# Six blocks of a shared expert taken in pairs, with stage 2 on its own after every two units

## The chip, the cores and the metric

The kernel runs on one core of a Trainium2 chip, in fp32. The metric is the device time of one execution in microseconds. Three executions of the kernel before took 1153.5, 1155.28 and 1156.86 us; the median is 1155.28 us. A further execution was recorded by the profiler; it took 1156.11 us.

The engines are named as in the profile: PE is the matrix engine TensorE, PEld its loading of weights, DVE is VectorE, ACT is ScalarE, POOL is GpSimd, and SP is SyncE, which here issues most of the DMAs.

## The reference

The input is `x` of 4 sequences x 1024 tokens x 512 features, and one condition vector of 512 for each sequence. Two residual layers follow one another:

```python
# layer 0: a linear map whose input is scaled by the condition
ys = cond / sqrt(512);  d = rsqrt((ys * ys) @ (W * W) + eps)
x  = x + ((x * ys) @ W) * d
# layer 1: a mixture of 8 routed experts, 2 for each token, and a shared one
shared = (silu(xf @ w1) * (xf @ w3)) @ w2            # 512 -> 1024 -> 512
s      = sigmoid(concat([xf, tf]) @ router_W)         # (4096, 8)
topk_idx = top_k(s + router_bias, 2)
gates  = s_sel / (s_sel.sum() + 1e-9)
h      = gelu(xf @ W1e[e]);  y = h @ W2e[e]           # 512 -> 512 -> 512
x      = x + (shared + sum of gates * y) / 3
```

The part that the change touches is `shared`, for 3072 of the 4096 tokens.

## The kernel before

**Blocks and phases.** The 4096 tokens are `NB` = 8 blocks of `TB` = 512. Layer 0 and the logits of the router run first, to about 132 us. Then comes the shared expert of the first six blocks (`early` = 6; blocks 6 and 7 are kept for the end), from 132 to 565 us. Meanwhile the router's choices are worked out on DVE and the tokens' rows are sorted by expert through DRAM. The routed experts follow (class `Double`, which does two groups of 256 rows at once, and class `Slot`), to about 1003 us, and last the two late blocks of the shared expert, under which the routed rows are gathered back.

**Seven products.** Every matrix product is cut in 2 x 2 blocks and made of seven block products instead of eight, as Strassen and Winograd do. Products 1, 6, 5 and 3 are added one after another in one PSUM bank, the chain, which is read out between them; products 2, 7 and 4 go to other banks (2 in one, 7 and later 4 in another). The sums of blocks that the scheme needs (of weights, of tokens, of hidden values) are made on DVE: `weight_sums` (L435), `token_sums` (L418), `hidden_sums` in `Shared`, `out_sums` (L897).

**A unit.** `Shared(blk, u)` takes one block and 256 of the 1024 hidden columns, of both `w1` (the gate, i = 0) and `w3` (the value, i = 1); there are four units a block (`HU` = 4). In stage 1 the two halves of the token side are the first and last 256 tokens of the block (`LO`, `HI`), and a bank of 512 columns holds the gate in one half and the value in the other. So each of the seven products is 2 matrices x 2 pieces of the contraction (`KH` = 2) = 4 matmuls of 256 columns. ACT copies the chain out (`evict`, L985), DVE adds the other banks (`add`, L989), ACT applies silu, and DVE multiplies gate and value to the hidden values.

**Stage 2** of a unit (`parts`, `seconds`, `drain`, L1052 to L1092) is the product with `w2`, 14 matmuls of 256 columns. It is cut in four parts, which `Shared.rest` (L991) issues between the products of the next unit's stage 1. Products 2, 7 and 4 of stage 2 add up over the four units of a block in PSUM; the chain is drained into the tiles `base` (which begin with x) four times in each unit, the three others once in each block, by DVE's `scalar_tensor_tensor` at L1092.

**What sets the order.** The order is written out by hand (`tc.manual_schedule()`): each engine runs its instructions in the order in which the program emits them, and waits by semaphores for the data. In every unit there are two points, `task(2 * self.at)` and `task(2 * self.at + 1)`, at which the program emits whatever the table `tasks` (L1573 to L1625) names for that point:

- the router's work: `sigmoid`, `pick_first`, `pick_second`, `count` (L735), `across`, `slots_of_experts` (L751), `positions`, `take_positions`, `gates`, `norm_gates`;
- sums of weights and of tokens for later units;
- DMAs on SP: `fetch_pairs` loads `base`, `fill` clears the sorted rows, `stage_rows` brings rows in, `fetch_first`, `fetch_second` and `load_rows` bring weights and rows of the first experts; on ACT's queue, `clear_rows`; on POOL's, `move_rows`, which scatters rows by index after a small copy on DVE;
- transposes (`turn_half`, L1153) and sums for the first `Double`.

**PSUM.** There are eight banks: four in the pool `ps_a`, handed out in turn (`bank_a`), used by stage 1, and four single ones, b0 to b3 (`bank_b`), used by stage 2 and, before it, by the logits: the logits of a block by chunk (`logits_by_chunk`, L376, tile `pq`) and their sum over chunks (`fold_logits`, L393, tile `pr`), to which DVE adds the condition's share at L399.

**The first Double.** `Double.rest` (L1251 on) issues the stage 2 of the unit before it, there the last `Shared` unit of block 5, between its own products, like `Shared.rest`. The driver's loop over all units is L1627 to L1670.

Of the kernel before, what the change touches and what calls it, by code (L numbers as in the profile page):

```python
# [45 lines left out]
def kernel(  # L46
# [328 lines left out]

    def logits_by_chunk(blk):  # L376

        pq = bank_b(f"pq{blk}")
        for k in range(KC):
            nc.tensor.matmul(  # L380
                pq[ts(k, Q)],
                lhsT=rw_pad[:, k, :],
                rhs=x1T[blk][:, k, :],
                start=True,
                stop=True,
                tile_position=(0, k * Q),
            )
        partial[blk] = late2.tile([P, TB], FP, tag="partial", name=f"partial{blk}")
        nc.scalar.activation(partial[blk], pq, AF.Copy)
# [2 lines left out]

    def fold_logits(blk, s):  # L393
        if s == 0:
            prs[blk] = bank_b(f"pr{blk}")
        nc.tensor.matmul(prs[blk][:, ds(s * E, E)], lhsT=partial[blk][:, ts(s, P)], rhs=fold, start=True, stop=True)
        if s == NS - 1:
            b = blk // BPB
            nc.vector.tensor_tensor(  # L399
                score[:, ts(blk, NS), :],  # L400
                prs[blk][:, : NS * E].rearrange("p (s e) -> p s e", e=E),
                t_logit[:, b : b + 1, :].to_broadcast([P, NS, E]),
                ALU.add,
            )
# [13 lines left out]
    def token_sums(blk):  # L418
        b = x1T[blk]
        k1, k2 = slice(0, KH), slice(KH, KC)  # L420
        v = t_tiles[blk % 2].rearrange("p (n k t) -> p n k t", n=3, k=KH)
        t1, t2, t4 = (v[:, n] for n in range(3))
        sub = lambda o, i0, i1: nc.vector.tensor_tensor(o, i0, i1, ALU.subtract)
        if blk not in begun:
            token_sum(blk)
        nc.vector.tensor_tensor(t2, b[:, k1, HI], b[:, k1, LO], ALU.add)
        sub(t1, b[:, k2, HI], t2)
        sub(t4, b[:, k2, LO], t2)
        t_of[blk] = (t1, t2, b[:, k1, HI], t4)

    def s_views(i, u):
        n = KH * P
# [163 lines left out]
    for blk in range(NB):  # L596
# [65 lines left out]
        if blk == early - 1:  # L662
            weight_sums(0)
        if blk == early:
            token_sums(0)
        if blk == NB - 1:
            weight_sums(1)
            nc.gpsimd.memset(zeros, 0.0)
# [12 lines left out]
    def open_pools():  # L681
        lin_ctx.close()
        later["row"] = ctx.enter_context(tc.tile_pool(name="row", bufs=4))
        sums = ctx.enter_context(tc.tile_pool(name="sums", bufs=1))
        more = sums.tile([P, 10 * TH], FP, name="more")
        work = ctx.enter_context(tc.tile_pool(name="work", bufs=1))
        t_tiles.append(sums.tile([P, 3 * KH * TH], FP, name="t1"))
        hgh = work.tile([P, 4, 2 * TB], FP, name="hgh")
        spot = [hgh[:, 3, ts(n, TH)] for n in range(4)]
        later["hs"] = spot[:3]  # L690
        later["more"] = [more[:, ts(n, TH)] for n in range(10)] + [spot[3], falling.rearrange("p t e -> p (t e)")]
        wide2 = lambda ap: ap.rearrange("p (q t) -> p q t", q=2)
        later["h2"] = [hgh[:, 2 * i : 2 * i + 2, :].rearrange("p q (m t) -> p q m t", m=2) for i in range(2)]
        later["s_w"] = [more[:, ts(n, 2 * TH)].rearrange("p (k q c) -> p k q c", k=KH, q=2) for n in range(3)]
        later["s_h"] = [wide2(more[:, ts(n, 2 * TH)]) for n in (3, 4)] + [wide2(zeros)]
        later["both"] = [hgh[:, i : i + 2, :].rearrange("p i (m t) -> p i m t", m=2) for i in range(2)]
        later["g"] = hgh[:, 1, :]
        later["h"] = [hgh[:, 2 * i, :] for i in range(2)]
# [193 lines left out]
    def out_tiles(u):  # L892
        return later["more"][3 * u : 3 * u + 3]
# [3 lines left out]
    def out_sums(u):  # L897
        t1, t2, t4 = out_tiles(u)
        b1, b2 = w2_sb[:, 2 * u, :], w2_sb[:, 2 * u + 1, :]
        b11, b12, b21, b22 = b1[:, LO], b1[:, HI], b2[:, LO], b2[:, HI]  # L900
        if u not in summed:
            nc.vector.tensor_tensor(b12, b22, b12, ALU.subtract)
            summed.add(u)
        nc.vector.tensor_tensor(t2, b12, b11, ALU.add)
        nc.vector.tensor_tensor(t1, b22, t2, ALU.subtract)
        nc.vector.tensor_tensor(t4, b21, t2, ALU.subtract)

    class Shared:

# [230 lines left out]
    def fetch_weights(j):  # L1140
        fetch_first(j)
        fetch_second(j)
# [16 lines left out]
    class Double:  # L1159
# [99 lines left out]
        def rest(self, prev, task):  # L1259
            j, h = self.j, later["h2"][self.j % 2]  # L1260
            self.h = h
            parts = [lambda mm=mm, drain=drain: (mm(), drain()) for mm, drain in prev.parts()]
            following = None if self.last else units[self.at + 1]
            self.evict(0, LO)
            self.product(self.chain, 6, False)
# [15 lines left out]
            parts[1]()  # L1281
            if following:
                following.sums_of_tokens((3, 2, 1))
            self.product(self.chain, 3, False)
            nc.scalar.activation(h[:, :, 0, HI], self.chain, AF.Gelu)
            nc.scalar.activation(h[:, :, 0, LO], h[:, :, 0, LO], AF.Gelu)
# [1 line left out]
            if following:  # L1288
                following.sums_of_first()
            task(2 * self.at)  # L1290
            self.product(self.seven, 4, False)
            self.add(self.seven, 1, LO)
            nc.scalar.activation(h[:, :, 1, :], h[:, :, 1, :], AF.Gelu)
            self.sums_of_second()
# [232 lines left out]
    def open_slot_pools():  # L1527
        rt_ctx.close()
        slot = ctx.enter_context(tc.tile_pool(name="slot", bufs=1))
        xg0 = slot.tile([P, KC, GS], FP, name="xg0")  # L1530
        xg1 = t_tiles[1][:, : KC * GS].rearrange("p (k t) -> p k t", k=KC)
        later["xg"] = [xg0, xg1]
        later["segs"] = slot.tile([P, 3 * SEGS, P], FP, name="xsegs")
        later["xseg"] = [later["segs"][:, ts(i, SEGS), :] for i in range(3)]

# [16 lines left out]
            nc.vector.transpose(big[0][:, k, :], later["segs"][:, : TB // Q, ts(k, Q)])  # L1552
        fetch_pairs(last_blk, [spare_pair(m) for m in range(2)])

    units = [Shared(blk, u) for blk in range(early) for u in range(HU)]
    units += [Double(j) for j in range(PAIRED)]
    units += [Slot(j) for j in range(SINGLE, SURE)]
    late = len(units)
    units += [Shared(blk, u) for blk in range(early, NB) for u in range(HU)]

    for i, unit in enumerate(units):
        unit.at = i
    tasks = {i: [] for i in range(2 * len(units))}

    def run_tasks(i):
# [5 lines left out]
        nc.scalar.dma_start(out=ys_d[ds(SURE * GS + i * P, P)], in_=zeros)  # L1571

    for u, work in (  # L1573
        (0, [lambda: out_sums(0)]),
        (1, [lambda: weight_sums(3, (0,))]),
        (2, [lambda: weight_sums(3, (1,)), lambda: out_sums(1)]),
        (3, [sigmoid, pick_first]),
        (4, [pick_second]),
        (5, [lambda: out_sums(2), count]),
        (6, [across, slots_of_experts]),  # L1580
        (7, [lambda: out_sums(3), positions]),
        (8, [load_spare, take_positions]),
        (9, [gates]),
        (10, [norm_gates]),
        (8 * HU + 1, [lambda: fetch_weights(0)]),
        (6 * HU + 4, [open_slot_pools]),
        (10 * HU + 1, [lambda: fetch_first(2)]),
        (10 * HU + 4, [lambda: fetch_second(2)]),
        (10 * HU + 4, [lambda: turn_half(0), lambda: load_rows(3)]),
        (10 * HU + 5, [lambda: turn_half(1), lambda: load_rows(4)]),  # L1590
        (10 * HU + 6, [lambda: units[early * HU].sums_of_first((1, 2))]),
        (10 * HU + 7, [lambda: units[early * HU].sums_of_tokens((3, 2))]),
        (10 * HU + 7, [lambda: units[early * HU].sums_of_first((7, 4))]),
        (10 * HU + 7, [lambda: units[early * HU].sums_of_tokens((1, 4))]),
        (2 * late, [reload_last, lambda: out_sums(0)]),
        (2 * late + 1, [lambda: out_sums(1)]),
        (2 * late + 3, [lambda: out_sums(2)]),
        (2 * late + 6, [lambda: out_sums(3)]),
        (2 * late - 1, [lambda: token_sum(early)]),
        (2 * late + 3, [turn_last]),  # L1600
        (2 * late + 5, [lambda: token_sums(last_blk)]),
        (2 * (late + HU + 1), [reload_w2]),
    ):
        tasks[u] += work
    for i in range((NSLOT - SURE) * SUB):
        tasks[6 * HU + 4 + i].append(lambda i=i: clear_rows(i))
    for i in range(ROWS // FILL):
        tasks[1 + i // 2].append(lambda i=i: fill(i))
    for m in range(NT // 2):
        tasks[9 + 2 * m].append(lambda m=m: stage_rows(m))  # L1610
        for i in range(2):
            tasks[10 + 2 * m + i].append(lambda t=2 * m + i: move_rows(t))
    for j in range(3):
        tasks[10 * HU + 2 + j].append(lambda j=j: load_rows(j))
    for blk in range(1, early):
        tasks[2 * blk * HU - 3].append(lambda blk=blk: token_sums(blk))
    for blk in range(early):
        tasks[2 * blk * HU].append(lambda blk=blk: fetch_pairs(blk))
    mine = list(range(early * NS))
    mine = [early * NS + i for i in range(NS)] + mine[:-NS] + list(range(NT - NS, NT)) + mine[-NS:]  # L1620
    points = 4 * TAIL * HU
# [4 lines left out]

    for s in range(NS):  # L1627
        fold_logits(NB - 2, s)
    units[0].begin()
    logits_by_chunk(NB - 1)  # L1630
    units[0].sevens()
    for s in range(NS):
        fold_logits(NB - 1, s)
    weight_sums(2)
    open_pools()
    prev = None
    for u, unit in enumerate(units):
        if u == late:
            for n in tc.Switch(later["spare"], E):
                prev.end = SURE + n  # L1640
# [19 lines left out]
        if u == late:  # L1660
# [1 line left out]
            base[early] = [spare_pair(2), pair_tile("base1")]  # L1662
            token_sums(early)
            unit.sevens()
        if prev is None:
            unit.rest(prev, run_tasks, units[u + 1])
        else:
            unit.rest(prev, run_tasks)
# [41 lines left out]
```

## Time and profile before

| what | value |
|---|---|
| median of three executions | 1155.28 us (1153.5 to 1156.86) |
| profiled execution | 1156.11 us, its span 1154.3 us |
| PE busy in the span | 1135.5 us (98%), 5222 records |
| DVE busy | 735.1 us (64%), 1533 instructions |
| ACT busy | 246.5 us (21%), 455 instructions |
| POOL busy | 181.8 us (16%), 222 instructions |
| granted PE clock, mean | 0.997 |
| first matmul of the first early unit | 132 us |
| first matmul of the first Double | 565 us |

The span is the time from the first to the last instruction in the profile; the execution's own time is 1.8 us more. The busy time of an engine is the sum of its instructions; an fp32 matmul leaves two records on PE and two weight loads. Names like L940 are lines of the kernel; L940 is the matmul of stage 1 and L1076 that of stage 2, in all eight blocks. In the timeline, equal neighbouring instructions are drawn together as "x8", and a square bracket behind a line tells how long the engine stood idle before it and which engine, tile and line let it go.

### The profile page before, as it was taken

What the parts mean: (1) busy time and instruction counts of PE and PEld (TensorE: products, weight loads), DVE (VectorE), ACT (ScalarE), POOL (GpSimd) and SP (SyncE); (2) the same over time, 40 slices, a digit from 0 to 9 for tenths busy, and PEclk for the clock granted to TensorE, in tenths of its full rate; (3) what the DMA queues carried; (4) which work ended last, traced back from release to release, by engine and by line L of the source; (5) the groups of instructions that cost most, each with busy time, mean ns of one, the idle gap of its engine ahead of it and who ended that gap; (6) DMA issues with size and microseconds to landing.
All of it is one profiled execution on the core that took longest, in us unless ns stands there. A gap on an engine that the chain in (4) does not pass through costs nothing. (4 is left out here: it accounts for less than half of the span.)

```text
span 1154.3 us, 14608 instructions
## 1 busy us (share of the span) xinstructions
PE 1135.5 (98%) x5222; PEld 974.4 (84%) x5222; DVE 735.1 (64%) x1533; ACT 246.5 (21%) x455; POOL 181.8 (16%) x222
## 2 busy tenths in 40 slices
PE   9899999999999999999999999999999998999998
PEld 6588888888888888888888888888888887888886
DVE  4688777854545445454687766677635554379987
ACT  2133231111111111111122222222222221121111
POOL 2000000022212222120000000000201100086850
PEclk9999999999999999999999999999999998999999
DMA  9698698322433337444356776657789983198971
GB/s 172 121 204 198 174 394 325 110 74 110 146 110 128 109 128 249 144 154 101 66 128 166 207 182 157 164 156 211 183 204 243 234 231 112 66 268 296 300 262 73
DMA packets 139393, 203.68 MB, mean 176 GB/s; under 512 B 9892, under 2 KB 67364, under 8 KB 139304
## 3 DMA queue, kind: packets, MB, share of 16 engines
q1 hardware_dynamic: 113096, 142.77, 44.6%
q0 software_dynamic: 14784, 47.24, 12.9%
q10 hardware_dynamic: 11424, 12.59, 3.8%
q8 instruction: 44, 0.72, 0.3%
q14 instruction: 45, 0.37, 0.1%
HBM read 120.76 MB, written 81.79 MB: 175 GB/s over the span
## 5 line engine op out<-in xcount | busy, mean ns | idle before, releaser
L1092 DVE SCALAR_TENSOR_TENSOR base<-s,base 128x512 f32<-128x512 f32 x131 | 88.7, 687 | 77.5 <-PE s L1076 77.4
L1076 PE MATMUL s<-w_sb,hgh 128*128 128x256 f32 x496 | 122.7, 380 | 1.9 <-DVE base L1092 1.9
L985 ACT ACTIVATE hgh<-ch 128x512 f32<-128x512 f32 x96 | 57.3, 596 | 273.8 <-PE ch L940 266.0
L878 POOL DMA_INDIRECT x1s_d<-big,addr x64 | 64.3, 1005 | 320.0 <-DVE addr L877 310.2
L1076 PEld LDWEIGHTS s<-w_sb,hgh 128*128 128x128 f32 x496 | 94.0, 190 | 16.1 <-DVE base L1092 3.5
L989 DVE TENSOR_TENSOR hgh<-se,hgh 128x512 f32<-128x512 f32 x64 | 44.1, 689 | 71.2 <-ACT hgh L985 62.3
L1512 POOL DMA_INDIRECT big<-ys_d,addr x64 | 71.8, 1122 | 104.9 <-DVE addr L1511 87.4
L125 POOL DMA_DIRECT2D xsegs<-x1s_d x40 | 23.2, 588 | 388.3 <-DVE big L1157 296.5
L1076 PE MATMUL s<-more,hgh 128*128 128x256 f32 x316 | 81.3, 380 | 0.9 <-DVE xsegs L1092 0.9
L1357 DVE TENSOR_TENSOR yd<-d,yd 128x512 f32<-128x512 f32 x36 | 24.8, 690 | 71.4 <-ACT yd L1353 39.1
L1076 PEld LDWEIGHTS s<-more,hgh 128*128 128x128 f32 x316 | 59.9, 190 | 9.6 <-DVE xsegs L1092 1.3
L1340 PE MATMUL d<-big,hgh 128*128 128x256 f32 x288 | 66.1, 379 | 0.0
L940 PE MATMUL ch<-w0t,seg 128*128 128x256 f32 x256 | 61.0, 381 | 1.0 <-ACT hgh L985 1.0
L1340 PEld LDWEIGHTS d<-big,hgh 128*128 128x128 f32 x288 | 54.8, 190 | 7.4
L940 PE MATMUL ch<-t,seg 128*128 128x256 f32 x256 | 60.5, 379 | 0.0
L940 PEld LDWEIGHTS ch<-w0t,seg 128*128 128x128 f32 x256 | 48.3, 190 | 8.9 <-ACT hgh L985 2.6
L940 PEld LDWEIGHTS ch<-t,seg 128*128 128x128 f32 x256 | 48.7, 190 | 6.5
L940 PE MATMUL se<-big,w_sb 128*128 128x256 f32 x224 | 53.0, 380 | 0.0
L940 PE MATMUL ch<-big,w_sb 128*128 128x256 f32 x224 | 53.0, 380 | 0.0
L940 PE MATMUL ch<-big,seg 128*128 128x256 f32 x224 | 52.9, 379 | 0.0
L940 PE MATMUL tw<-big,w_sb 128*128 128x256 f32 x224 | 52.9, 379 | 0.0
L940 PEld LDWEIGHTS se<-big,w_sb 128*128 128x128 f32 x224 | 42.6, 190 | 6.5 <-issue 0.8
(300 smaller groups left out, 2129.9 us busy)
## 6 DMA issues: line engine op xcount, KB each, us to landing
big<-in_L_cond_W1e_dram SPq DMA_DIRECT2D x88, 256.0 KB, 5.8
big<-in_L_cond_W2e_dram SPq DMA_DIRECT2D x22, 1024.0 KB, 5.6
x1s_d<-w0t SPq DMA_DIRECT2D x13, 1536.0 KB, 16.8
xsegs<-x1s_d SPq DMA_DIRECT2D x96, 128.0 KB, 3.2
ys_d<-yd SPq DMA_DIRECT2D x24, 512.0 KB, 4.3
x_d<-back SPq DMA_DIRECT2D x32, 256.0 KB, 4.4
big<-x_d SPq DMA_DIRECT2D x16, 512.0 KB, 3.7
base<-x_d SPq DMA_DIRECT2D x12, 512.0 KB, 4.6
```

Source lines behind the costliest of these rows:

```text
L125: eng.dma_start(out=tile_ap[ts(g, Q)], in_=v[g])
L878: ins = nc.gpsimd.indirect_dma_start(out=x1s_d, out_offset=bass.IndirectOffsetOnAxis(ap=at.bitcast(U32), axis=0), in_=staged(t // 2)[:, t ...
L940: nc.tensor.matmul(out, lhsT=lhs[:, k, :], rhs=rhs[:, k, :], start=start and k == 0, stop=k == KH - 1, skip_group_check=not start,)
L985: nc.scalar.activation(self.both[:, :, m, cols], self.chain, AF.Copy)
L989: nc.vector.tensor_tensor(r, bank, r, ALU.add)
L1076: nc.tensor.matmul(out[:, s], lhsT=a[:, ts(s, P)], rhs=b, start=start and s == 0, stop=True, skip_group_check=not (start and s == 0),)
L1092: nc.vector.scalar_tensor_tensor(r, bank, third, r, ALU.mult, ALU.add)
L1340: nc.tensor.matmul(out[:, i], lhsT=a[:, q, ts(i, P)], rhs=b[:, q, :], start=start and i == 0 and q == 0, stop=q == 1, skip_group_check=not ...
L1357: nc.vector.tensor_tensor(r, bank, r, ALU.add)
L1512: nc.gpsimd.indirect_dma_start(out=picks[t][i], out_offset=None, in_=ys_d, in_offset=bass.IndirectOffsetOnAxis(ap=at.bitcast(U32), axis=0) ...
```

## The change

The six early blocks are taken as three pairs. A new class `Pass` takes one matrix (the gate of unit u, then its value) for two blocks at once: the two halves of the token side in stage 1 are now the two blocks of the pair, 512 tokens each, instead of the halves of one block. A pass has 14 matmuls of 512 columns; there are 24 passes. Between its own chain products it issues products 1 and 2 of the next pass. Its banks are pinned: the chain takes b0 and b3 in turn, product 2 takes b1, products 7 and 4 take b2. The sums over the two blocks (`both_sums`) replace `token_sums` for these blocks.

Stage 2 no longer lies between the products of a stage 1. After every two units (four passes) a `Second` for each of the two blocks does it for both units at once: 28 matmuls of 256 columns, with seven drains on DVE. The first is begun in the fourth pass, by two halves of products 1 and 2 in the place of the next pass's; `Second.run` does the rest of the first block with pieces of the second between, and `Second.parts` does what is left of the second. Stage 2 takes its banks from `ps_a`, and adds nothing up in PSUM over more than two units.

The points for tasks are now 72 rounds, 24 for each pair and 12 for every two units: eight in the four passes, two in `run`, two in `parts`. Tasks are placed anew on them; `sigmoid` stands on round 4, `count` with half of `weight_sums(3)` on 7, `across` and `slots_of_experts` on 9. `weight_sums(2)`, which stood ahead of the first unit, becomes two tasks. The `base` tiles of both blocks of a pair are fetched together. Tiles are laid out anew (`hgh` has six rows instead of four; `more` nine tiles instead of ten), and the last logits take bank b3.

The first `Double` has no stage 2 of another unit to issue between its products, and issues its product 4 ahead of its product 3. The late blocks stay in class `Shared`.

```diff
     def logits_by_chunk(blk):
-        pq = bank_b(f"pq{blk}")
+        pq = bank_b(f"pq{blk}", 3 if blk == NB - 1 else None)
...
-            prs[blk] = bank_b(f"pr{blk}")
+            prs[blk] = bank_b(f"pr{blk}", 3 if blk >= NB - 2 else None)
...
+    def both_sums(p, names):
+        a, b = x1T[2 * p], x1T[2 * p + 1]
+        sub = lambda o, i0, i1: nc.vector.tensor_tensor(o, i0, i1, ALU.subtract)
+        for n, k in names:
+            if n == 3:
+                sub(b[:, k, :], b[:, KH + k, :], b[:, k, :])
+            if n == 2:
+                nc.vector.tensor_tensor(both_t(2, k), b[:, k, :], a[:, k, :], ALU.add)
+            if n == 1:
+                sub(both_t(1, k), b[:, KH + k, :], both_t(2, k))
+            if n == 4:
+                sub(both_t(4, k), a[:, KH + k, :], both_t(2, k))
...
+    class Pass:
...
+        def product(self, out, n, start):
+            u, w = self.u, w13[self.i]
+            a, b = x1T[2 * self.p], x1T[2 * self.p + 1]
...
+                1: (w[:, :KH, c1], lambda k: a[:, k, :]),
+                2: (w[:, KH:, c1], lambda k: a[:, KH + k, :]),
+                3: (s4, lambda k: b[:, KH + k, :]),
+                4: (w[:, KH:, c2], lambda k: both_t(4, k)),
+                5: (s1, lambda k: both_t(1, k)),
+                6: (s2, lambda k: both_t(2, k)),
+                7: (w[:, :KH, c2], lambda k: b[:, k, :]),
...
+        def rest(self, fillers, task, following=None, closing=None):
+            if not self.taken:
+                self.evict(0, 0)
+            self.product(self.chain, 6, False)
+            if not self.has_seven:
+                self.sevens()
+            self.add(self.two, 0, 0)
+            self.evict(1, 0)
+            fillers[0]()
+            task()
+            self.product(self.chain, 5, False)
+            self.evict(1, 1)
+            self.add(self.seven, 1, 1)
+            fillers[1]()
+            self.product(self.chain, 3, False)
+            self.close(0, ts(0, TB))
+            self.close(0, ts(1, TB), self.chain)
+            if closing:
+                closing.sum(3)
+            self.product(self.seven, 4, False)
+            self.add(self.seven, 1, 0)
+            if following:
+                following.evict(0, 0)
+                following.taken = True
+                self.close(1, slice(0, 2 * TB))
+            else:
+                self.close(1, ts(0, TB))
+                self.close(1, ts(1, TB))
+            task()
+
+    class Second:
...
+        def run(self, other, task):
+
+            self.first(1)
+            self.drain(self.chain, 0, LO)
+            self.seven = self.bank("ss")
+            self.product(self.seven, 7, True)
+            self.sum(1)
+            self.sum(2)
+            self.second(1)
+            other.first(0)
+            self.product(self.chain, 6, False)
+            self.drain(self.two, 0, LO)
+            self.drain(self.chain, 1, LO)
+            task()
+            other.first(1)
+            self.drain(self.seven, 1, HI)
+            self.product(self.chain, 5, False)
+            self.sum(4)
+            self.drain(self.chain, 1, HI)
+            other.sum(3)
+            self.product(self.seven, 4, False)
+            other.sum(1)
+            other.sum(2)
+            self.product(self.chain, 3, False)
+            self.drain(self.seven, 1, LO)
+            other.drain(other.chain, 0, LO)
+            self.drain(self.chain, 0, HI)
+            other.sum(4)
...
+            task()
...
+        def seconds(self, part):
+            if part == 0:
+                self.seven = self.bank("ss")
+                self.product(self.seven, 7, True)
+            if part == 1:
+                self.product(self.chain, 6, False)
+                self.second(0)
+                self.second(1)
+            if part == 2:
+                self.product(self.chain, 5, False)
+            if part == 3:
+                self.product(self.seven, 4, False)
+                self.product(self.chain, 3, False)
+
+        def take(self, part):
+            if part == 0:
+                self.drain(self.seven, 1, HI)
+            if part == 1:
+                self.drain(self.chain, 1, LO)
+                self.drain(self.two, 0, LO)
...
     class Double:
...
+            if not prev:
+                self.product(self.seven, 4, False)
             self.product(self.chain, 3, False)
...
+    on(4, sigmoid, pick_first)
+    on(5, lambda: weight_sums(2, (1,)), pick_second)
+    on(7, count, lambda: weight_sums(3, (0,)))
+    on(9, across, slots_of_experts)
...
+    for p in range(PAIRS):
+        on(p * ROUND + 2, lambda p=p: fetch_pairs(2 * p), lambda p=p: fetch_pairs(2 * p + 1))
+        if p + 1 < PAIRS:
+            on(p * ROUND + 18, lambda p=p: both_sums(p + 1, ((3, 0), (3, 1))))
+            on(p * ROUND + 20, lambda p=p: both_sums(p + 1, ((2, 0), (2, 1))))
+            on(p * ROUND + 21, lambda p=p: both_sums(p + 1, ((1, 0), (1, 1))))
+            on(p * ROUND + 22, lambda p=p: both_sums(p + 1, ((4, 0), (4, 1))))
...
+    on(68, lambda: turn_half(0), lambda: load_rows(3))
+    on(69, lambda: turn_half(1), lambda: load_rows(4))
...
+    for at, one in enumerate(passes):
+        if at % 4 == 0 and at > 0:
+            one.begin()
+        if not one.closes:
+            nxt = passes[at + 1]
+            one.rest((nxt.begin_chain, nxt.begin_two), next_round, following=nxt)
+            continue
+        two = [Second(2 * one.p + i, one.u - 1) for i in range(2)]
+        one.rest((lambda: two[0].first(0), lambda: two[0].second(0)), next_round, closing=two[0])
+        two[0].run(two[1], next_round)
+        for i, (mm, drain) in enumerate(two[1].parts()):
+            mm()
+            drain()
+            if i in (1, 3):
+                next_round()
```

## The prediction

> **What bounds the kernel now.** I read the page first: engines, then stretches of the span, then single instructions.
>
> ```profile
> span 1154.3 us, 14608 instructions
> PE 1135.5 (98%) x5222; PEld 974.4 (84%) x5222; DVE 735.1 (64%) x1533; ACT 246.5 (21%) x455; POOL 181.8 (16%) x222
> ```
>
> TensorE (PE) is busy 98% of the span, so only two things move the time: what a matmul takes, and whether PE stands still. The table of stretches (from:to, length, then busy time and count of PE, weight loads, DVE, ACT, POOL, then granted clock, DMA share, GB/s) says so of the stage that is changed, which runs from 131 to 565 us:
>
> ```profile
> 350.00:400.00 50.00, 50.00 (x233) 44.08 (x232) 22.57 (x49) 8.11 (x17) 9.89 (x11) 1.00 0.32 111
> 131.00:590.00 459.00, 457.40 (x2127) 400.92 (x2126) 267.93 (x598) 84.87 (x157) 64.85 (x65) 1.00 0.46 155
> ```
>
> 50.00 of 50 us busy: here PE never waits, and all other work is hidden. In 131 to 590 only 1.6 us are idle. The timeline (start, length of the group, what it is; in brackets the idle time before it and its releaser) shows where, and gives the prices of waits:
>
> ```profile
> 49.49 0.67 PE L527 MATMUL chl<-t_lin,x1T 128*128 128x256 f32 x2 [2.60 <-DVE x1T L488]
> ...
> 135.60 1.07 PE L380 MATMUL pq<-x1T,rw_pad 128*32 128x512 f32 x8
> 136.27 0.18 DVE L399 TENSOR_TENSOR score<-pr,t_logit 128x32 f32<-128x32 f32 x1
> ...
> 147.95 1.89 PE L940 MATMUL se<-w0t,w_sb 128*128 128x256 f32 x8
> 150.01 1.13 PE L940 MATMUL ch<-w0t,seg 128*128 128x256 f32 x4 [0.17 <-ACT hgh L985]
> ...
> 166.78 1.28 ACT L716 ACT_TABLE_LOAD   x1
> 169.03 0.92 PE L940 MATMUL ch<-w0t,seg 128*128 128x256 f32 x3 [0.63 <-ACT hgh L985]
> ...
> 189.17 0.61 DVE L737 TENSOR_TENSOR picked<-one,two 128x256 f32<-128x256 f32 x1
> 190.83 0.69 DVE L415 TENSOR_TENSOR big<-big 128x512 f32<-128x512 f32 x1
> ...
> 199.51 0.16 DVE L755 TENSOR_TENSOR shift<-pp,last 128x8 f32<-128x8 f32 x1
> 203.20 0.67 DVE L989 TENSOR_TENSOR hgh<-se,hgh 128x512 f32<-128x512 f32 x1
> ...
> 303.40 1.03 PE L1076 MATMUL s<-w_sb,hgh 128*128 128x256 f32 x4
> 303.60 0.60 ACT L985 ACTIVATE hgh<-ch 128x512 f32<-128x512 f32 x1 [4.58 <-PE ch L940]
> ...
> 569.02 1.97 PE L1236 MATMUL chd<-t,more 128*128 128x256 f32 x8 [0.42 <-DVE t L1173]
> 582.73 1.13 PE L1076 MATMUL s<-w_sb,hgh 128*128 128x256 f32 x4 [0.39 <-DVE base L1092]
> ...
> 964.30 3.75 PE L1385 MATMUL ph<-xg,big 128*128 128x256 f32 x8 [3.90 <-issue]
> ...
> 1140.78 1.28 DVE L1092 SCALAR_TENSOR_TENSOR xsegs<-s,xsegs 128x512 f32<-128x512 f32 x2
> 1143.35 7.03 PE L1102 MATMUL f<-w_sb,hgh 128*128 128x512 f32 x16
> ```
>
> Prices from them. Eight records of 256 columns take 1.89 us and the last alone 0.38, so one starts every (1.89 − 0.38)/7 = 0.2157 us. Sixteen of 512 columns take 7.03, the last 0.59: one every 0.429 us. (Each fp32 matmul is two records.) A product of the scheme takes 8 × 0.2157 = 1.73 us, half of one 0.86; four 512-wide records 1.72. From PE's last start slot to the consumer's start is 0.20 (303.40 to 303.60). An eviction is 0.60, a DVE operation on 128x512 0.69; two independent ones start 0.60 apart (1.28 − 0.68). A producer's end to PE's next start is 0.05, and the first group after a wait is 0.10 longer (1.13 against 1.03).
>
> **The change part by part.** I follow PE's new order and ask of each product whether its producers end before PE arrives.
>
> *Rate.* The early six blocks have 24 units of 28 matmuls, 1344 records of 256 columns; they become 672 of 512. Each pair saves 2 × 0.2157 − 0.4292 = 0.0022 us: −1.5 us. Rounding of the two rows allows 0 to −3.
>
> *Stage-2 arithmetic* stays the same on PE. DVE's drains into base fall from 6 × 20 = 120 to 12 × 7 = 84, which saves 36 × 0.69 = 25 us of DVE, worth nothing where DVE is hidden.
>
> *Stalls that go.* 150.01 (0.17 idle, and smaller ones with it: 0.43) and 169.03 (0.63 plus others: 0.89): ACT's evictions late, the second behind the 1.28 us table load of sigmoid. In a pass two products of 1.72 us lie between the eviction and the next chain product, so these go: −1.3 us. Late next there is the following pass's first eviction, one product ahead: covered too.
>
> *A. Start.* The logits of the last block now share the pinned bank b3 with the score addition of the block before (L399), which ends at 136.45 behind eight weight sums on DVE. The logits' matmuls start at 135.60 now, then at 136.5: +0.9. Bounds 0 (if DVE has less ahead of it) and 1.5.
>
> *B. Closing pass* (each second value pass, six times): its fillers are halves of a stage-2 product, 0.86 instead of 1.72 us. Chain product 3 waits for the eviction of product 5: 0.20 + 0.60 + 0.15 = 0.95 against 0.86: 6 × 0.09 = +0.5.
>
> *C. Second.run*: product 5 waits for the drain of product 6: 0.20 + 0.69 + 0.15 = 1.04, with 0.86 of cover: 6 × 0.18 = +1.1.
>
> *D. Second.run, product 6* needs the hidden sums 1 and 2, made on DVE after stage 1's last addition. From the end of the last stage-1 product: addition 0.20 to 0.89, two closing multiplications from 0.92 to 2.21, drain from 2.13, sum 1 from 2.73, sum 2 from 3.45 to 4.14, PE at 4.30. PE has 0.86 + 1.73 + 0.86 + 0.86 = 4.31 of other work. Covered by 0.02 us, so anything more that DVE does in between is paid for in full. Row-copy rounds cost perhaps 0.1 twice: +0.2.
>
> *E. Token sums of the next pair, and the first Double's transposes,* stand before drains in three halves: about 0.08 each: +0.2.
>
> *F. Round 7,* at the end of the first closing pass, puts count and the weight sums of one matrix into D's chain. Count takes 190.83 − 189.17 = 1.66; the weight sums 1.43 (133.37 to 134.80, at the start). Less the margin, sum 2 is 3.0 us late, and PE idles that long before product 6: +3.0. Before, count stood between two units where 1.73 us products covered it.
>
> *G. Round 9* runs slots_of_experts (203.20 − 199.51 = 3.7 us of small DVE operations, one after another) just before the second half's drains. Product 5 of that half waits for the second drain: 0.20 + 1.20 + 3.7 + 0.60 + 0.69 + 0.15 = 6.5 us after the last product of the first half; PE has three products, 5.2: +1.3.
>
> *H. First Doubles.* Without a stage 2 beside it, the first Double moves product 4 ahead of product 3; it waits for eviction and addition: 0.20 + 0.60 + 0.03 + 0.69 + 0.15 = 1.67 us with nothing between. The second Double's product 6 waits for an eviction behind the first's gelu, about 1.3. Now these two units idle 1.6 (569.02, 582.73 and three smaller): +1.4.
>
> The passes' other waits have 1.72 us of cover. fetch_pairs, stage_rows, move_rows and clear_rows move by a few microseconds on the SP, POOL and ACT queues; their users come tens of microseconds later, so 0, and a few tenths each where a transfer ran into the next.
>
> Sum: −1.5 − 1.3 + 0.9 + 0.5 + 1.1 + 0.2 + 0.2 + 3.0 + 1.3 + 1.4 = +5.8 us on the profiled execution's 1156.1, which is 0.8 above the median of 1155.28: 1161.1 us.
>
> *The clock.* F's stall is the longest before PE. At 49.49 PE had idled 2.60 us and went on at full rate; at 964.30 it had idled 3.90 and eight records took 3.75 instead of 1.89; some twelve records ran at half rate, 2.5 us lost. F lies between. [...] I take no loss of clock, and keep 2.5 for the range.
>
> **The rivals.**
> 1. *DVE has slack at F or G.* If part of the 1.66, 1.43 and 3.7 us was waiting and not work, or DVE reaches those rounds earlier than I count, F and G shrink by up to 4.3: 1156.8. For it: DVE is only 58% busy in 131 to 590. Against: the order is written by hand, and the sums and drains stand behind the rounds on DVE. With A and H also milder, 1155.5. Chance 0.19.
> 2. *DVE becomes the bound in every half.* D has 0.02 us of margin; each half that is 0.6 (one operation) late costs six times that, +3.6; or the clock falls at F, +2.5: 1163.6 to 1164.7, both 1167. For it: 4.30 against 4.31; against: the rows are medians of quiet places. Chance 0.20.
> 3. *The other side: 512 columns are faster than the row.* Saving 9.3 us to reach 1151.8 needs 9.3/672 = 14 ns per record more, so one every 0.415 us in place of 0.429; with F and G covered, 7.5 ns or 0.422. For it: weight loads (0.19 us each) get twice the time to hide. Against: 350 to 400 us shows no load that holds PE up (233 records in 50 us is one every 0.215), and the 512-wide row is 0.429 in this kernel. If it came, about 1151. Chance 0.07.
>
> **How the numbers follow.** My forecast 0.54, the rivals 0.19, 0.20, 0.07. A measurement tells about 0.3% (3.5 us) from no change. The forecast (+5.8) and rival 2 lie above: slower 0.74. Rival 1 (0.2 to 3 us above) lies within: 0.19. Rival 3: faster 0.07. The range reaches from rival 1's low end, 1155.5, to rival 2's both-sided end with a little for E and the queues, 1168; the forecast's own, with A from 0 to 1.5 and the rate from 0 to −3, is 1158.7 to 1163.2.
>
> **What would show it.** Right: 512-wide records of stage 1 about 0.43 apart; one idle of about 3 us on PE before product 6 in the first half, released by a hidden sum; gaps of 0.1 to 0.2 in each run before product 5, released by a drain; about 1.3 us early in the first second half; 1.7 and 1.3 at the first two Doubles; nothing in stage 1's passes; DVE some 25 us less busy. Wrong: gaps inside the passes, a gap before product 6 in all six halves, half-rate records after F, or no gap at F.

## The result, and the profile after

The changed kernel takes 1161.95 us (median of six executions, 1160.13 to 1164.53); the kernel before took 1155.44 us in six executions on the same chip. The ratio is 1.0055, with a 95% interval of 1.0043 to 1.0067: slower by 0.5%, some 6.4 us. The forecast was 1161.1. The profiled execution took 1163.95 us.

The page of the changed kernel, its first lines and the row of the granted clock:

```profile
span 1162.2 us, 13093 instructions
PE 1138.3 (98%) x4550; PEld 845.6 (73%) x4550; DVE 699.9 (60%) x1419; ACT 239.1 (21%) x419; POOL 178.7 (15%) x222
PEclk9999998999999999999999999999999999999999
```

PE has 672 records fewer, as counted; what that is worth, 1.6 us, e6_halves shows below. DVE is 35 us less busy, 25 of them the fewer drains into `base`, as forecast; PE was never idle from 350 to 400 us before, so there this can have shortened nothing. The 8 in the clock row is the seventh slice, 174 to 203 us, where the first stage 2 lies. Before, that slice had a 9 and an 8 stood near 965 us, at the first `Slot`. The table of stretches (the columns are those of the prediction) has one undisturbed stretch and this one:

```profile
350.00:400.00 50.00, 50.00 (x142) 26.68 (x141) 14.69 (x37) 8.87 (x15) 15.56 (x16) 1.00 0.38 127
186.00:200.00 14.00, 11.16 (x38) 8.99 (x37) 8.59 (x19) 0.00 (x0) 0.00 (x0) 0.76 0.59 219
```

From 350 to 400 us PE is as full as it was before. From 186 to 200 it is idle for 2.84 us, and the granted clock is 0.76 on the average. What PE waited for from 131 to 600 us, by the list of waits (total, times, longest):

```profile
PE sc L1076 <- DVE hgh L1055: 2.8, 1, 2.8
PE sed L1489 <- DVE hgh L1510: 1.4, 1, 1.4
PE chd L1489 <- ACT hgh L1506: 1.1, 1, 1.1
PE pq L380 <- DVE score L399: 0.9, 1, 0.9
PE sc L1076 <- DVE base L1082: 0.9, 1, 0.9
```

These are steps F, H (two lines), A and G of the prediction, each with the releaser that it named. (The list gives idle time; from start to start, as in the table further down, a wait counts some 0.16 us more, and F's 2.84 is 3.00.) The first one in the timeline, PE and then DVE:

```profile
188.29 1.03 PE L1076 MATMUL sc<-w_sb,hgh 128*128 128x256 f32 x4
192.16 3.78 PE L1076 MATMUL sc<-more,hgh 128*128 128x256 f32 x8 [2.84 <-DVE hgh L1055]
195.73 1.91 PE L1076 MATMUL sc<-w_sb,hgh 128*128 128x256 f32 x4
```

```profile
186.97 0.60 DVE L763 TENSOR_TENSOR picked<-one,two 128x256 f32<-128x256 f32 x1
...
188.63 0.42 DVE L459 TENSOR_TENSOR seg<-w_sb 128x256 f32<-128x256 f32 x1
...
190.09 0.68 DVE L1082 SCALAR_TENSOR_TENSOR base<-sc,base 128x512 f32<-128x512 f32 x1
190.69 1.41 DVE L1055 TENSOR_TENSOR hgh<-hgh 128x512 f32<-128x512 f32 x2
```

DVE does count from 186.97 and the four weight sums from 188.63; only then, at 190.09, the drain and at 190.69 the two hidden sums that product 6 needs. They end at 192.10, and PE starts at 192.16. Then eight records take 3.78 us in place of 1.99: the clock has halved (the granted clock is 0.50 from 191.56 to 198.38). That second loss, 3.1 us until full rate is back at 198.39, the forecast had kept for the range only.

The six executions of the changed kernel differ chiefly in how long the clock was down. Their mean granted clocks are on record: 0.998 at 1160.13 and 1160.59 us, 0.996 at 1161.47 and 1162.43, 0.995 at 1163.95 and 1164.53. A mean clock lower by 0.003 is 3.5 us of the span, nearly all of the 3.9 us between the two shortest and the two longest; a mean doesn't tell, though, at which wait the clock fell.

### The profile page after: what moved, and what is told of

Read it like the earlier page. It is cut to its first block, busy times and chain, and to the rows that moved or that the text cites. A ratio compares the mean times of both kernels' runs of the same rounds, so it can differ in the third digit from the quotient of the medians.

```text
span 1162.2 us, 13093 instructions
## 1 busy us (share of the span) xinstructions
PE 1138.3 (98%) x4550; PEld 845.6 (73%) x4550; DVE 699.9 (60%) x1419; ACT 239.1 (21%) x419; POOL 178.7 (15%) x222
## 5 line engine op out<-in xcount | busy, mean ns | idle before, releaser
L962 PE MATMUL pc<-w0t,seg 128*128 128x512 f32 x144 | 69.7, 593 | 0.0
L1598 PE MATMUL d<-w0t,hgh 128*128 128x256 f32 x288 | 68.0, 379 | 0.0
L1598 PEld LDWEIGHTS d<-w0t,hgh 128*128 128x128 f32 x288 | 54.7, 190 | 7.4
L1076 PE MATMUL sc<-w_sb,hgh 128*128 128x256 f32 x192 | 48.2, 384 | 0.0
L1082 DVE SCALAR_TENSOR_TENSOR base<-sc,base 128x512 f32<-128x512 f32 x48 | 32.4, 685 | 26.1 <-PE sc L1076 26.1
L1489 PE MATMUL chd<-t,more 128*128 128x256 f32 x192 | 45.5, 380 | 1.1 <-ACT hgh L1506 1.1
L962 PE MATMUL pc<-big,seg 128*128 128x512 f32 x96 | 45.7, 598 | 0.0
L962 PE MATMUL ps<-big,w_sb 128*128 128x512 f32 x96 | 45.2, 593 | 0.0
L962 PE MATMUL pc<-big,w_sb 128*128 128x512 f32 x96 | 45.2, 593 | 0.0
L962 PE MATMUL pt<-big,w_sb 128*128 128x512 f32 x96 | 45.1, 592 | 0.0
L962 PE MATMUL ps<-t,w_sb 128*128 128x512 f32 x96 | 45.1, 592 | 0.0
```

The source lines that it names most:

```text
L962: nc.tensor.matmul(out, lhsT=lhs[:, k, :], rhs=rhs(k), start=start and k == 0, stop=k == KH - 1, skip_group_check=not start,)
L1076: nc.tensor.matmul(out[:, i], lhsT=a[:, q, ts(i, P)], rhs=b, start=first, stop=True, skip_group_check=not first)
L1082: nc.vector.scalar_tensor_tensor(r, bank, third, r, ALU.mult, ALU.add)
L1489: nc.tensor.matmul(bank[:, q], lhsT=lhs[:, k, q, :], rhs=rhs[:, k, :], start=start and q == 0 and k == 0, stop=k == KH - 1, skip_group_che ...
L1598: nc.tensor.matmul(out[:, i], lhsT=a[:, q, ts(i, P)], rhs=b[:, q, :], start=start and i == 0 and q == 0, stop=q == 1, skip_group_check=not ...
```

## The experiments

All kernels below differ from the changed kernel as shown, and were compared with the kernel before on one chip; so ratios are compared, not times.

### Round 7 emptied (e1_round7)

```diff
-    on(7, count, lambda: weight_sums(3, (0,)))
+    on(6, count)
+    on(11, lambda: weight_sums(3, (0,)))
```

> The changed kernel with count moved from round 7 to round 6 and the weight sums of one matrix from round 7 to round 11; nothing else. In the changed kernel's profile matmul stands idle 2.84 us before product 6 of the first Second.run, released by a hidden sum, and the next fourteen records start 0.427 us apart instead of 0.216. Theory (step F, DVE's order at the end of the first closing pass): the gap goes down to the 0.02 us margin of the other halves, and with it the half-rate records; so 3.0 us of waiting and, in executions in which the clock had fallen, another 3.1: profile 1157.8 us, median 1156 to 1159. Rival 1 (DVE has no room for these 3.1 us elsewhere either): the wait comes back at round 6 or 11 as a gap of 1 to 3 us in the closing pass or at the next pass's product 6, and the time stays above 1160. Rival 2 (the half rate has another cause than the idle time): the gap goes, the slow records stay somewhere, 1159 to 1161.

Measured: 1158.24 us, ratio 1.0013 (1.0005 to 1.0022), against 1.0055 with the work in round 7: 0.42%, 4.9 us less. Of the list of waits (131 to 600 us) the first line is gone, and the others stand unchanged:

```profile
PE sed L1489 <- DVE hgh L1510: 1.4, 1, 1.4
PE chd L1489 <- ACT hgh L1506: 1.1, 1, 1.1
PE pq L380 <- DVE score L399: 0.9, 1, 0.9
PE sc L1076 <- DVE base L1082: 0.9, 1, 0.9
```

No record between 142 and 964 us starts at half rate. So DVE did have room for these 3.1 us at rounds 6 and 11, and rival 1 of the expectation falls; what cost time was the place. The gap of 3.0 us and the half rate go together: rival 2 falls too. The profiled execution took 1160.92, not 1157.8, for two reasons that lie outside the change. Its first pass began 1.7 us later than the changed kernel's, most of it because the clock fell at a gap in layer 0; here is that gap in the changed kernel and in e1_round7:

```profile
49.30 1.97 PE L545 MATMUL chl<-t_lin,x1T 128*128 128x256 f32 x8 [2.61 <-DVE x1T L506]
```

```profile
49.55 3.38 PE L545 MATMUL chl<-t_lin,x1T 128*128 128x256 f32 x8 [2.60 <-DVE x1T L506]
```

And the wait ahead of the first `Slot` (from 965 us), with the clock falling there in both, was 1.2 us dearer.

### Round 9 emptied (e2_round9)

```diff
-    on(9, across, slots_of_experts)
+    on(9, across)
+    on(11, slots_of_experts)
```

> The changed kernel with slots_of_experts moved from round 9 to round 11, past the second half's drains; nothing else. In the changed kernel's profile product 5 of the first second half waits 0.88 us (1.15 with the slower restart) for a drain behind that group. Theory (step G): the gap goes, nothing replaces it, 1.1 us less: median 1160.8, and the gap of step F with its half-rate records stays. Rival (the group only moves its wait into the next pass, whose additions then stand behind 3.7 us of DVE): no gain, a gap of about 1 us after product 5 of the third unit's first pass.

The line with `base` L1082 is gone from the list of waits, and nothing has come in its place in the next pass; the rest is as in the changed kernel. In time, 1162.51 us and a ratio of 1.0050 (1.0034 to 1.0066) against 1.0055 (1.0043 to 1.0067): 0.6 us less, which the intervals can't tell from 0 or from 1.1. The trace shows that G was a real wait of 1.05 us; the timing doesn't resolve it.

### Cover for the first two Doubles (e3_double)

```diff
     first Double.rest:
+            if not prev:
+                turn_half(2 * j + 3)
+                load_rows(2 * j + 6)
+                following.sums_of_tokens((3, 2))
+                following.sums_of_first((7,))
...
+            if not prev:
+                following.begin_two()
-            if not prev:
-                self.product(self.seven, 4, False)
             self.product(self.chain, 3, False)
...
+            self.product(self.seven, 4, False)
     second Double.begin: products 1 and 7 in place of 1 and 2
```

> The changed kernel with cover for the first two Doubles: product 2 of the second Double is issued between products 5 and 3 of the first, product 7 of the second takes its place, product 4 of the first stands behind product 3 again, and the second's transposes and token sums come ahead of the first's later additions on DVE. In the changed kernel's profile these two units idle 1.41 and 1.11 us (1.58 and 1.28 from start to start, 0.10 more each at the restart). Theory (step H): both go, because each chain read has a product of 1.73 us beside it: 2.9 us less, median 1159.0. Rival (DVE is full there: with the second's transposes first, the first's additions come late, and a gap of 1 us or more stands before product 4 of the first or product 6 of the second): 1160 to 1162.

Measured: 1159.09 us, ratio 1.0024 (1.0012 to 1.0037): 0.31%, 3.6 us less by the ratios, where 2.9 was expected; the two intervals allow either. The list of waits has lost the two lines of the Doubles and nothing else:

```profile
PE sc L1076 <- DVE hgh L1055: 2.8, 1, 2.8
PE pq L380 <- DVE score L399: 0.9, 1, 0.9
PE sc L1076 <- DVE base L1082: 0.9, 1, 0.9
```

So H was a lack of cover, not a lack of DVE time.

### The small gaps alone (e7_small)

```diff
-        pq = bank_b(f"pq{blk}", 3 if blk == NB - 1 else None)
+        pq = bank_a(f"pq{blk}") if blk == NB - 1 else bank_b(f"pq{blk}")
...
     Second.run:
             other.first(0)
+            if following:
+                following.begin_chain()
+                following.evict(0, 0)
+                following.taken = True
             self.product(self.chain, 6, False)
...
             other.first(1)
+            if following:
+                following.begin_two()
...
-        if at % 4 == 0 and at > 0:
-            one.begin()
...
-        one.rest((lambda: two[0].first(0), lambda: two[0].second(0)), next_round, closing=two[0])
+        one.rest((lambda: None, lambda: (two[0].first(0), two[0].second(0))), next_round, closing=two[0])
```

> The changed kernel with only the cover of steps A to E: last logits in a bank of the other pool, both fillers of the closing pass between products 5 and 3, products 1 and 2 of the next pass inside Second.run ahead of its products 6 and 5. Round 7, round 9 and the first Doubles stay as they are. Theory: A's 0.95 us, B's six gaps of 0.09 (0.5) and the small gaps in five of the six runs (1.2) go; the gap of F shrinks by the 1.72 us of product 1, to 1.3 us, which is under 2 us in any stretch, so the clock no longer falls there (0.0 instead of 3.1 us in two executions of three): 1.0 + 0.5 + 1.2 + 1.7 + 2.1 = 6.5 us, median 1155.4, ratio to the kernel before 1.000; G and H stay (1.05 and 1.6 + 1.3 from start to start). Rival (the small gaps are a margin that any cover only moves): new gaps of the same sum at the next pass's product 6; 1158 to 1159.

Measured: 1156.83 us, ratio 1.0005 (0.9993 to 1.0016), 0.5% below the changed kernel and level with the kernel before, as expected. The stretch of the first stage 2 shows why so much came back from a few small covers:

```profile
186.00:200.00 14.00, 12.88 (x53) 9.52 (x52) 9.81 (x20) 0.60 (x1) 0.00 (x0) 1.00 0.75 280
```

F's gap has shrunk to 1.1 us, though round 7 stands where it stood, and the clock stays at 1.00. A is gone, and so are B's six gaps and all the gaps of C, D and E but those of the last half, which has no next pass to borrow from.

### All of it (e4_all, e5_spare)

e4_all has the edits of the four kernels above. e5_spare has one more:

```diff
-    on(12, positions, load_spare)
+    on(12, positions)
...
-    on(14, gates, lambda: weight_sums(3, (1,)))
+    on(14, load_spare, gates, lambda: weight_sums(3, (1,)))
```

> All waits of the list taken away at once: the moves of the three runs before it, the last logits in a bank of the other pool (step A), both fillers of the closing pass between products 5 and 3 (step B), and products 1 and 2 of the next pass inside Second.run, ahead of its products 6 and 5 (steps C, D, E). Theory (the waits A to H are all that the change costs, and the rate of 512 columns and the two old stalls are what it brings): 1.5 of rate, 1.3 of old stalls in stage 1 and 1.6 at the first two Doubles below the kernel before, so median 1151.0, and matmul idle less than 0.5 us between 141 and 600 us. Rival (pairs of blocks make DVE or ACT late by themselves, so that waits taken away come back elsewhere): above 1154.5, with new gaps in the passes. Rival (512 columns bring nothing): about 1152.5 with no gaps.

> The kernel with all waits taken away, and the loading of spare into the engines' registers moved from round 12 to round 14. In that kernel's profile matmul still idles 1.29 us at 216.75, put down to spare (L810): the register load stands in matmul's own queue right behind slots_of_experts, which now runs at round 11. Theory: that gap goes, 1.45 us from start to start, and nothing replaces it: median 1149.8, ratio to the kernel before 0.9942. Rival (the gap is the additions behind slots_of_experts on DVE, not the register load): it stays at 1.3 and the median at 1151.3.

e4_all took 1151.31 us, ratio 0.9955 (0.9940 to 0.9970): faster than both kernels. One new wait came up, at 216.75 us:

```profile
PE pc L962 <- DVE spare L810: 1.3, 1, 1.3
```

PE itself loads the number `spare` into a register at round 12, and slots_of_experts, which makes it, now ran at round 11; PE's queue stood behind the load. In e5_spare that wait is gone:

```profile
131.00:590.00 459.00, 459.00 (x1474) 276.28 (x1473) 236.54 (x491) 78.18 (x123) 63.72 (x65) 1.00 0.48 159
```

459.00 of 459 us busy; the kernel before had 457.40. Its median, 1152.16 us (ratio 0.9970, 0.9958 to 0.9983), doesn't show the 1.4 us; the two intervals overlap, and the expected ratio of 0.9942 lies outside e5_spare's. (In e5_spare's profile the clock fell at the first `Slot`, where eight records took 3.48 us, in e4_all's it didn't, 1.97.) Both are faster than the kernel before; which of the two is the faster stays open.

### 256 columns in place of 512 (e6_halves)

This is e5_spare with each 512-wide matmul of the passes issued as two:

```diff
-            for k in range(KH):
-                nc.tensor.matmul(out, lhsT=lhs[:, k, :], rhs=rhs(k), ...)
+            for spot, half in enumerate((LO, HI)):
+                for k in range(KH):
+                    nc.tensor.matmul(out[:, half], lhsT=lhs[:, k, :], rhs=rhs(k)[:, half], ...)
```

> The same kernel as in the run beside it, but every matmul of 512 columns in the passes issued as two of 256 columns, with the same weights loaded twice; nothing else. Theory (step rate: two records of 256 columns take 2.2 ns more than one of 512): 672 x 2.2 ns = 1.5 us more, profile and median alike, and no new idle time. Rival 3 of the prediction (512 columns hide the weight loads, and bring several microseconds): 5 to 9 us more. Rival (nothing): the same time within 0.3 us in the profile of stage 1.

From product 6 of the first pass to the last product 6 of stage 2 in the last run (rows of 512 columns first, then of 256):

```profile
139.56 1.96 PE L962 MATMUL pc<-w0t,seg 128*128 128x512 f32 x4
...
553.12 0.70 PE L1076 MATMUL sc<-more,hgh 128*128 128x256 f32 x2
```

```profile
141.10 1.97 PE L963 MATMUL pc<-w0t,seg 128*128 128x256 f32 x8
...
556.26 0.70 PE L1077 MATMUL sc<-more,hgh 128*128 128x256 f32 x2
```

413.56 against 415.16 us: 1.60 us for the 512 columns, with PE full in both. The medians (1152.16 and 1152.45) are too close to tell. So the rate is worth what the prediction had (1.5 us), and rival 3 of the prediction falls.

### The clock, with gaps made to measure (c2_delay19, c1_delay26, c3_delay33)

e1_round7 with useless additions on an unused tile, ahead of the drain and the sums, in five of the six halves; the computation is unchanged. They ask how far the length of a gap tells whether the clock falls. The list reads `[TB] * 2 + [TH] * 1` in c2_delay19 and `[TB] * 4 + [TH] * 1` in c3_delay33; the lines that make the tile `pad` are left out.

```diff
...
+    def delay():
+        pad = later["pad"]
+        for n in [TB] * 3 + [TH] * 1:
+            nc.vector.tensor_tensor(pad[:, :n], pad[:, :n], pad[:, :n], ALU.add)
+    for i in range(5):
+        on(7 + 12 * i, delay)
```

> The changed kernel with round 7's work moved as in the first run, and in its place at the end of the closing pass of five halves (rounds 7, 19, 31, 43, 55) useless additions on an unused tile, 3 x 0.72 + 0.45 = 2.6 us, on DVE ahead of the drain and the sums: matmul then idles about 2.6 us before product 6 in each. [...] Rival (any idle time over 2.5 us is enough): 5 of 5.

> The same with 4 x 0.72 + 0.45 = 3.3 us of useless additions in each of the five halves. [...] Rival (a threshold on the idle time itself at 3 us): 5 of 5.

> The kernel of the two runs with useless additions, with 2 x 0.72 + 0.45 = 1.9 us of them in each of the five halves; matmul should idle 1.7 to 1.8 us before product 6. [...]

Stretches of 10 us around the five gaps (the figure behind POOL's count is the granted clock; 0.83 is half rate for 3.4 of the 10 us). The lengths of the gaps go from start to start. Gaps of 1.7 to 1.8 us (c2):

```profile
189.00:199.00 10.00, 8.49 (x39) 6.93 (x38) 7.55 (x14) 0.00 (x0) 0.00 (x0) 1.00 0.53 201
265.00:275.00 10.00, 8.50 (x38) 6.78 (x37) 8.45 (x14) 0.00 (x0) 0.00 (x0) 1.00 0.01 2
339.00:349.00 10.00, 8.37 (x38) 6.83 (x37) 7.67 (x15) 0.00 (x0) 2.98 (x4) 1.00 0.45 159
413.00:423.00 10.00, 8.37 (x38) 6.54 (x37) 8.41 (x17) 0.00 (x0) 3.41 (x4) 1.00 0.39 137
488.00:498.00 10.00, 8.50 (x39) 6.93 (x38) 7.56 (x13) 0.00 (x0) 0.00 (x0) 1.00 0.76 157
```

Gaps of 2.4 to 2.5 us (c1):

```profile
190.00:200.00 10.00, 7.77 (x35) 6.27 (x35) 7.52 (x13) 0.00 (x0) 0.00 (x0) 1.00 0.56 212
267.00:277.00 10.00, 7.77 (x29) 6.22 (x28) 7.26 (x13) 0.00 (x0) 0.00 (x0) 0.83 0.01 2
343.00:353.00 10.00, 7.65 (x28) 5.94 (x27) 6.13 (x13) 0.00 (x0) 3.24 (x4) 0.83 0.34 127
420.00:430.00 10.00, 7.64 (x34) 5.89 (x34) 8.45 (x16) 0.00 (x0) 3.09 (x3) 1.00 0.37 132
495.00:505.00 10.00, 7.77 (x29) 6.22 (x28) 6.02 (x11) 0.00 (x0) 0.00 (x0) 0.83 0.63 157
```

Gaps of 3.1 to 3.2 us (c3):

```profile
190.00:200.00 10.00, 7.04 (x32) 5.64 (x31) 7.48 (x13) 0.00 (x0) 0.00 (x0) 1.00 0.61 231
268.00:278.00 10.00, 7.04 (x24) 5.20 (x23) 6.72 (x12) 0.00 (x0) 0.00 (x0) 0.83 0.01 2
345.00:355.00 10.00, 6.92 (x24) 5.47 (x24) 6.58 (x13) 0.00 (x0) 3.12 (x4) 0.83 0.33 120
423.00:433.00 10.00, 6.92 (x31) 5.27 (x30) 8.41 (x17) 0.00 (x0) 3.06 (x3) 1.00 0.36 131
499.00:509.00 10.00, 7.04 (x25) 5.58 (x24) 6.02 (x11) 0.00 (x0) 0.00 (x0) 0.83 0.82 157
```

The clock fell in 0, 3 and 3 of 5. c3_delay33's gaps, all over 3 us, cost it in three cases of five, so both rivals with 5 of 5 fall (c1_delay26's own gaps came out at 2.4 to 2.5 us, no longer than the 2.5 that its rival names). Equal gaps do and don't cost the clock, and the longer ones do it no more often in this small number.

## Why the prediction was right, and where it was not

| step | forecast, us | measured, us |
|---|---|---|
| rate | −1.5 | −1.6 (e6_halves) |
| old stalls of stage 1 | −1.3 | gone: no gap in stage 1's passes but B |
| A, start | +0.9 | 1.11 from start to start, 0.09 of it there before: +1.0 |
| B, closing passes | +0.5 | 6 x 0.09 = +0.5 |
| C, D, E, the runs and second halves | +1.5 | +1.6, in five of six halves |
| F, waiting | +3.0 | +3.0 |
| F, clock | 0, 2.5 in the range | +3.1 where it fell |
| G | +1.3 | +1.05, 1.15 with the restart |
| H, over the two gaps before | +1.4 | 1.58 + 1.28 from start to start: +1.3 |

**Right.** The way of working held: follow PE's order, and for each product add up what stands before its producer on DVE or ACT. All the gaps came where they were placed; the five that the list of waits shows have the releasers named, and B to E are too short for that list. The moved DMAs cost nothing that the list of waits from 131 to 600 us shows. That the pieces are causes and not only neighbours in time is shown by taking them away: F by e1_round7, G by e2_round9 (in the trace only), H by e3_double, A to E, and part of F with them, by e7_small; all of it together gives e4_all, 1151.31 us, for which the list alone, taken from the time before, had given 1151.0 (by the ratio, on the chip of the first result, 1150.2).

**G** was put 0.2 us too long. The drain that product 5 waits for ended 6.6 us after the last product of the first half, where the forecast had 6.5 with the restart in it; but PE had 0.36 us more to do in that time than the three products counted, the small matmuls of `across`.

**D** had a forecast margin of 0.02 us; apart from the first half, product 6 was on time in three halves and 0.10 us late in the two with row copies.

**Wrong: the clock at F.** The step that failed is "I take no loss of clock"; half-rate records after F stood among the prediction's own signs of being wrong. The time lost in waiting at F was right (3.00 us from start to start), and the clock fell on it in three of three profiles that have it (the changed kernel's, e2_round9's and e3_double's). The row of 2.60 us at full rate, taken as a lower end, and that of 3.90 us at half rate, taken as the upper, were read as lengths; length alone doesn't tell: the same gap of 2.6 us, in layer 0, cost the clock in six of the twelve profiles (e1_round7, e2_round9, e6_halves, e7_small, c1_delay26, c3_delay33). No run shows the zero that the sum has for the clock at F; in its place the changed kernel's profile showed 3.1 us. Nor does a run show the bound of "2 us in any stretch" in e7_small's expectation, which was its author's estimate; the runs showed a granted clock of 1.00 around e7_small's gap of 1.1 us and c2_delay19's of 1.7 to 1.8.

**The number.** The terms of the table, G with its restart, add up to some +5.7 us without the fall and +8.8 with it. The changed kernel's profile took 7.84 us more than before's; nearly all of the 1.0 between is the first `Slot`, where the wait and the half rate behind it cost 5.7 us in place of before's 6.6. The median, 1161.95, lies between the forecast without a fall (1161.1) and the profile with one (1163.95), as the granted clocks of the six executions do. That the forecast came within 0.9 us of the median is in this part luck: it left the fall out, and the fall came in a part of the executions.

**The rivals.** Rival 1 (slack at F or G): no, the sums stood behind the rounds. Rival 2 came true in the part of it that is the clock, and not in the part that every half is late. Rival 3 fell with e6_halves.

## What to carry to other kernels

Where one engine is full, a change of order is judged product by product: what stands ahead of its producer in that producer's own queue, and how much other work lies between. Work parked on a helper engine "somewhere idle" is free only at points with cover; here moving 3.1 us of DVE work to other rounds was worth 4.9 us, and lending products as cover in e7_small was worth 0.5%, which brought the change level with the kernel before; it took all the edits together to make it 0.3 to 0.45% faster. And a gap on PE cost its length and the 0.1 us of the restart in these runs (eight records took 1.99 us behind c1_delay26's first gap, 1.89 in an undisturbed place); where the clock fell, another 1.4 us (e1_round7's gap in layer 0, 3.38 us for eight records in place of 1.97) to 3.1 us (F). It fell behind none of c2_delay19's five gaps of 1.7 to 1.8 us, and behind six of the ten of 2.4 to 3.2 us in c1_delay26 and c3_delay33.

## What was not expected of the hardware

Gaps of one length can differ in whether the clock falls. c1_delay26's first two gaps, and c3_delay33's:

```profile
193.09 1.99 PE L1078 MATMUL sc<-more,hgh 128*128 128x256 f32 x8 [2.23 <-DVE hgh L1057]
...
269.71 0.70 PE L1078 MATMUL sc<-more,hgh 128*128 128x256 f32 x2 [2.23 <-DVE hgh L1057]
```

```profile
194.19 1.99 PE L1078 MATMUL sc<-more,hgh 128*128 128x256 f32 x8 [2.96 <-DVE hgh L1057]
...
271.53 1.17 PE L1078 MATMUL sc<-more,hgh 128*128 128x256 f32 x2 [2.96 <-DVE hgh L1057]
```

PE idled 2.23 us ahead of both in c1_delay26 and 2.96 ahead of both in c3_delay33. Around the first of each pair the granted clock was 1.00, around the second 0.83 (the rows of 10 us above). Nor does the longer gap cost more surely: c3_delay33's first, of 2.96, cost nothing of the clock, while F's of 2.84 and that of 2.60 in layer 0 of e1_round7 did.

How long half rate lasts; c1_delay26's second gap, and F in the changed kernel:

```profile
267.00:270.92 3.92, 1.69 (x9) 1.16 (x8) 3.19 (x6) 0.00 (x0) 0.00 (x0) 1.00 0.02 4
270.93:274.33 3.40, 3.40 (x10) 2.69 (x9) 1.95 (x4) 0.00 (x0) 0.00 (x0) 0.50 0.00 0
274.35:277.00 2.65, 2.65 (x14) 2.34 (x13) 2.10 (x4) 0.00 (x0) 0.00 (x0) 1.00 0.00 0
```

```profile
191.56:198.38 6.82, 6.22 (x15) 4.97 (x16) 3.03 (x5) 0.00 (x0) 0.00 (x0) 0.50 0.36 136
```

That is 3.40 us, and twice as much, 6.82, at F. There the clock fell at 191.56, while PE still stood idle, PE went on at 192.16, and full rate was back at 198.39.

What tells apart two gaps of one length is left open here. Six of the ten made gaps of 2.4 to 3.2 us cost the clock; six in ten is an estimate from them of how often F's 3.00 us does, and a reason why the changed kernel's six executions spread over 4.4 us, at mean granted clocks of 0.998 to 0.995.

A register load on PE's own queue was a wait that no matmul's operands showed: it held PE for 1.29 us in e4_all. When the work that makes such a number moves, the load has to move with it.
